# Graph attention: head 6 turned on VectorE in tiles 1 to 6, two turned heads copied by VectorE

## The chip, the core and the metric

The kernel runs on one core of a Trainium2 chip. The core has TensorE (PE; its weight loads are listed as PEld), VectorE (DVE), ScalarE (ACT), GpSimd (POOL) and SyncE (SP), each of which works through its own instructions in the order in which the program gives them; they meet at semaphores. Transfers are issued by SP and POOL and run on 16 DMA engines. The metric is the device time of one execution in microseconds (us); the verdict compares medians of runs.

## The reference

Two graph layers on x of 16 batches x 1024 nodes x 256 features, float32, with an adjacency matrix per batch. Layer 0 is masked attention with 8 heads of 32 features. Layer 1 scores pairs of nodes by one of four edge kinds.

```
h = relu(layernorm(x))
Q, K, V = h Wq' + bq, h Wk' + bk, h Wv' + bv          # 8 heads of 32
attn = softmax(where(adj == 0, -inf, Q K' / sqrt(32)))
x = x + (attn V) Wo' + bo                              # layer 0
h = relu(layernorm(x))
e_k = leaky_relu((h * a_k) h', 0.2),  k = 0..3
s = where(adj == 1, e_0, -9e15); where(adj == 2, e_1, s); ...
x = x + softmax(s) h                                   # layer 1
```

## The kernel before

**Tiles.** A tile is 128 nodes of one batch: 8 tiles a batch, 128 in all. The main loop takes one tile a turn (index s, tile t = s mod 8) and in it goes through eight stages h = 0 to 7, one head each. The order of the instructions on every engine is the order in which this loop writes them: nothing reorders them. Work of several tiles is interleaved in it: the heads of the present tile; the end of the last tile's layer 0; layer 1 of a tile nine turns back (the *edge* tile; from the tenth turn on); and the projections of a piece nine ahead.

**A head.** In stage h TensorE computes the scores of head h (`scores`, L460, two matmuls of 512 columns into PSUM). VectorE adds the mask and takes the maximum in the same instruction, into a tile `p` (`softmax_max`, L472), and reads its accumulator. In the next stage ScalarE takes the exponential, in place in `p` (`softmax_exp`, L489). In the one after, the probabilities are turned, so that the keys lie on the partitions. Heads 0 to 3 are combined with the values in stage 7 (`combine(0)`), heads 4 to 7 in stage 3 of the next turn (`combine(1)`, L524), on TensorE. Heads 6 and 7 thus have their turns in stages 0 and 1 of the next turn of the loop.

**Two ways of turning.** On TensorE: eight transpositions of 128x128 into PSUM (L588), and two copies of 128x512 into `pT` (`turn_half`, L589), by ScalarE. Or by blocks: VectorE transposes all 32x32 blocks in one instruction (`blocks_of`, L381) into a buffer `blocks`, and four transfers issued by SP (`placed`, L386, 128 KB each) put the blocks in their places in `pT`. The second way gives another order of the keys. Heads 0, 1, 4 and 5 (`MIXED`) have their values in the order that it wants, the other four in the natural order. `BY_BLOCKS` says which heads go by blocks in a tile; a tile that it does not list takes `MIXED`. Where a head's way does not agree with its values' order, the exponential does not work in place: it writes to a second `p`, with steps, so that the order comes out right (head 5 of tile 7, head 0 of tile 0).

**What is shared.** The scores of heads 4 and 6, and the edge tile's, use one PSUM side; all other heads use the other one. So scores h+1 wait, as a rule, for the maximum of head h. There are 4 buffers `p` (7 `pT`), and 3 `blocks`, given out in rotation; a buffer of `blocks` is free when the four transfers out of it have landed. The edge tile's layer 1 also goes by blocks: its probabilities (`sel`) are transposed on VectorE in stage 0, behind what the stage turns of the last tile's head 6 and ahead of stage 1's maximum.

**Stage 0 on the engines**, after the scores and the maximum of head 0: TensorE turns head 6 of the last tile, then computes the first half of the edge tile's scores (L624 transpositions, L630 matmuls; for edge tile t, between 1.9 us at t = 0 and 0.6 us from t = 4 on); VectorE transposes `sel`. In stage 1 TensorE does the scores of head 1, the turn of head 7, the turn of the normed nodes (L563) and the queries of a piece (L267); in stage 2 scores of head 2 come first. SP's transfers of stages 6 to 0 are, in order: head 4's four, a store of x (L550), head 5's four, the edge tile's four.

**Keys.** In tile 7 and tile 0 SP also loads the next batch's keys, 512 KB a head.

Of the kernel before, what the change touches and what calls it, by code (L numbers as in the profile page):

```python
# [24 lines left out]
NEG_INF = -9000000000000000.0  # L25
MASKED = -1e30
MIXED = (0, 1, 4, 5)
BY_BLOCKS = {7: (0, 1, 4), 0: (1, 4, 5)}


def by_blocks(t):
    return BY_BLOCKS.get(t, MIXED)

# [14 lines left out]
def gnn_kernel(  # L48
# [18 lines left out]
    nc = tc.nc  # L67
# [120 lines left out]
    class Piece:  # L188
# [39 lines left out]
        def turn(self):  # L228
            self.hT = self.buffer(2, [P, NC, self.n * P])
            self.hTm = self.buffer(4, [P, NC, self.n * P])  # L230
            for c in range(NC):
                if self.n > 1:
                    tr = ps_tr.tile([P, self.n, P], F32, tag="tr", name="trn0")
                elif c == 0:
                    tr = by_chunk(late)
                for t in range(self.n):
                    nc.tensor.transpose(
                        tr[:, c if self.n == 1 else t, :], self.h[:, t, c * P : (c + 1) * P], ident
                    )
                if self.n > 1:  # L240
                    nc.scalar.copy(self.hT[:, c, :], tr.rearrange("p t n -> p (t n)"))
                    nc.vector.tensor_copy(
                        self.hTm[:, c, :].rearrange("p (t k b) -> p t k b", t=self.n, b=NB),
                        tr.rearrange("p t (b k) -> p t k b", b=NB),
                    )
            self.h_ps = tr
# [168 lines left out]
    class Attend:  # L415
# [75 lines left out]
        def turn(self, h, half):  # L491
            if half == 0:
                self.turned[h] = ptp.tile([P, NT, P], F32, tag="pT", name="pT")
            turn_half(self.probs[h][0], self.turned[h], half)

        def turn_blocks(self, h):
            self.blocks = blocks_of(self.probs[h][0])
# [85 lines left out]
    def turn_half(p, pT, half, copy=nc.scalar.copy):  # L583

        tr = ps_tr.tile([P, 4, P], F32, tag="tr", name="trp")
        for j in range(4):
            jj = half * 4 + j
            nc.tensor.transpose(tr[:, j, :], p[:, jj * P : (jj + 1) * P], ident)  # L588
        copy(pT[:, half * 4 : half * 4 + 4, :], tr)  # L589
# [467 lines left out]
```

## Time and profile before

| | |
|---|---|
| median of 3 runs | 3100.66 us (3096.59 to 3105.06) |
| profiled execution | 3097.96 us, span 3096.2 us |
| granted TensorE clock | 0.992 on average |
| TensorE busy | 2943.1 us, 95% |
| VectorE, ScalarE, GpSimd busy | 2478.1, 2651.9, 2171.0 us (80%, 86%, 70%) |
| one tile, first maximum to first maximum of the next, mean of batches 1 to 14, tiles 0 to 7 | 26.1, 23.6, 23.1, 22.8, 22.6, 22.6, 22.2, 23.1 us |

A group's line reads: line of the kernel, engine, operation, output<-inputs, shape, count | busy us, mean ns of one | idle time of the engine just before them, and what ended it. A timeline's line reads: start (us from the span's start), length, engine, line, operation; in square brackets the idle time before and what released the engine. The busy time of matmuls is modelled, as they are pipelined.

### The profile page before, as it was taken

To read this page: it belongs to the slowest core of one execution; us is meant where nothing else is said; L and a number is where in the kernel's file an instruction comes from. 1 tells how busy PE (TensorE), PEld (TensorE's weight loads), DVE (VectorE), ACT (ScalarE), POOL (GpSimd) and SP (SyncE) were. 2 spreads that over 40 slices of the span, in tenths; PEclk is the share of its full clock that TensorE was granted. 3 is DMA by queue.
4 is the path that set the end of the run, shared out by engine and by line. 5 is a ranking of instruction groups with operands and counts; after the bars stand their busy time and mean duration, and the time that the engine had idled before them with its cause. 6 is when DMAs were issued, how large, how long until landed. Compare 5 with 4: busy or idle time off the path is not lost. (4 is left out here: it accounts for less than half of the span.)

```text
span 3096.2 us, 95999 instructions
## 1 busy us (share of the span) xinstructions
PE 2943.1 (95%) x36466; PEld 2211.1 (71%) x36466; DVE 2478.1 (80%) x4359; ACT 2651.9 (86%) x5221; POOL 2171.0 (70%) x2995
## 2 busy tenths in 40 slices
PE   5888999999999999999999999999999999999997
PEld 3666777777777777777777777777777777776663
DVE  3777878878787887878888788887878888787884
ACT  3888988988898988898989898898899988898882
POOL 2666777777777777777777777777777777776542
PEclk8999999999999999999999999999999999999999
DMA  5776777877778777787877878777787877778663
GB/s 203 216 237 210 225 250 229 252 219 234 251 217 275 212 235 236 236 252 227 266 219 234 257 220 272 217 230 253 227 256 225 263 226 234 253 224 255 182 175 99
DMA packets 616259, 712.44 MB, mean 230 GB/s; under 512 B 65328, under 2 KB 546992, under 8 KB 615792
## 3 DMA queue, kind: packets, MB, share of 16 engines
q1 hardware_dynamic: 546720, 494.08, 53.1%
q0 software_dynamic: 66960, 210.04, 20.9%
q8 instruction: 293, 4.80, 0.7%
q10 hardware_dynamic: 2112, 2.10, 0.2%
q14 instruction: 174, 1.43, 0.2%
HBM read 252.98 MB, written 134.22 MB: 125 GB/s over the span
## 5 line engine op out<-in xcount | busy, mean ns | idle before, releaser
L472 DVE CUSTOM_DVE_ANT_0 p<-s,neg 128x1024 f32<-128x1024 f32 x1024 | 1235.9, 1208 | 296.1 <-PE s L460 231.8
L489 ACT ACTIVATE p<-p,nmx 128x1024 f32<-128x1024 f32 x1024 | 1218.7, 1191 | 174.3 <-DVE nmx L472 172.2
L460 PE MATMUL s<-k,qt 128*128 128x512 f32 x2048 | 761.6, 453 | 70.8 <-DMA k<-kd 36.5
L589 ACT COPY pT<-trp 128x512 f32<-128x512 f32 x1088 | 581.9, 591 | 66.2 <-PE trp L588 64.1
L381 DVE STREAM_TRANSPOSE blocks<-p 128x1024 f32<-128x1024 f32 x488 | 603.9, 1238 | 14.5 <-ACT p L677 10.6
L588 PE MATMUL trp<-ident,p 128*128 128x128 f32 x4352 | 566.2, 273 | 1.7 <-ACT pT L589 1.2
L588 PEld LDWEIGHTS trp<-ident,p 128*128 128x128 f32 x4352 | 506.7, 141 | 83.3 <-ACT pT L589 9.1
L524 PE MATMUL acc<-pT,v 128*32 128x128 f32 x16384 | 536.0, 276 | 27.4 <-ACT recT L518 20.6
L524 PEld LDWEIGHTS acc<-pT,v 128*32 128x32 f32 x16384 | 456.2, 111 | 136.5 <-ACT recT L518 74.8
L440 POOL TENSOR_SCALAR neg<-adj 128x1024 bf16<-128x1024 int32 x128 | 467.7, 3654 | 80.3 <-ACT neg L452 71.1
L695 PE MATMUL acc<-h,pT 128*32 128x256 f32 x8192 | 494.7, 383 | 7.9 <-DVE ot L704 7.8
L460 PEld LDWEIGHTS s<-k,qt 128*128 128x128 f32 x2048 | 322.8, 191 | 173.9 <-issue 72.6
L695 PEld LDWEIGHTS acc<-h,pT 128*32 128x32 f32 x8192 | 241.6, 110 | 211.2 <-issue 64.4
L673 POOL TENSOR_TENSOR sel<-sel,less 128x1024 f32<-128x1024 f32 x120 | 286.8, 2390 | 76.6 <-ACT less L662 51.3
L630 PE MATMUL s<-h1T,ha 128*128 128x512 f32 (+2 forms) x744 | 272.8, 490 | 2.6 <-ACT h1T L567 1.3
L671 POOL TENSOR_SCALAR less<-top 128x1 f32<-128x1 f32 x120 | 31.6, 264 | 267.7 <-DVE top L653 267.6
L324 POOL DMA_DIRECT2D qd<-halves x240 | 177.0, 777 | 58.7 <-POOL halves L314 31.8
L489 ACT ACTIVATION_READ_ACCUMULATOR p<-p,nmx 128x1 f32 x1024 | 205.9, 201 | 0.0
L508 POOL COPY wide<-rec 128x256 f32<-128x256 f32 x128 | 53.9, 421 | 215.7 <-DVE rec L506 215.7
L330 POOL DMA_DIRECT2D kd<-halves x240 | 171.7, 764 | 35.4 <-POOL halves L314 35.4
L314 POOL TENSOR_TENSOR halves<-full,halves 128x256 fp32r<-128x256 f32 x240 | 176.4, 735 | 20.6
L630 PEld LDWEIGHTS s<-h1T,ha 128*128 128x128 f32 x744 | 126.7, 190 | 70.7 <-issue 45.0
(120 smaller groups left out, 4239.8 us busy)
## 6 DMA issues: line engine op xcount, KB each, us to landing
pT<-blocks SPq DMA_DIRECT2D x2432, 128.0 KB, 3.5
k<-kd SPq DMA_DIRECT2D x128, 512.0 KB, 6.5
qt<-qd SPq DMA_DIRECT2D x128, 512.0 KB, 4.5
adj<-in_adj POOLq DMA_DIRECT2D x127, 512.0 KB, 5.2
qd<-halves POOLq DMA_DIRECT2D x240, 256.0 KB, 3.1
kd<-halves POOLq DMA_DIRECT2D x240, 128.0 KB, 4.3
xb<-in_x POOLq DMA_DIRECT2D x128, 128.0 KB, 4.4
x1d<-x SPq DMA_DIRECT2D x128, 128.0 KB, 4.1
```

The lines of the kernel that those rows point to most:

```text
L324: nc.gpsimd.dma_start(out=qds[self.b][self.first, oc].rearrange("p u w n -> p u (w n)"), in_=halves.unsqueeze(1).to_broadcast([P, 2, 2 * P]),)
L381: nc.vector.transpose(blocks.rearrange("p b j q -> p j b q"), p)
L440: nc.gpsimd.tensor_scalar(self.neg, self.adj, 0.0, MASKED, ALU.is_equal, ALU.mult)
L460: nc.tensor.matmul(self.ps[:, cols], lhsT=self.qt[:, h, :], rhs=keysets[self.b][h][:, cols], start=True, stop=True,)
L472: nc.vector.tensor_tensor_reduce(out=p, in0=sides[h in (4, 6)], in1=self.neg, scale=-SCALE, scalar=FLOOR, op0=ALU.add, op1=ALU.min, accum_ ...
L489: nc.scalar.activation(to, of, AF.Exp, bias=nmx, scale=-1.0, accum_out=self.sums[:, h : h + 1])
L524: nc.tensor.matmul(sums_place[r * HD : (r + 1) * HD, g * P : (g + 1) * P], lhsT=vs[self.b][:, j, place_of(h) : place_of(h) + HD], rhs=self ...
L588: nc.tensor.transpose(tr[:, j, :], p[:, jj * P : (jj + 1) * P], ident)
L589: copy(pT[:, half * 4 : half * 4 + 4, :], tr)
L630: nc.tensor.matmul(self.side[:, cols], lhsT=self.ha[:, c, :], rhs=h1T[:, c, cols], start=(c == 0), stop=(c == NC - 1),)
L673: nc.gpsimd.tensor_tensor(self.sel, self.sel, self.less, ALU.subtract)
L695: nc.tensor.matmul(sums_place[a * HD : (a + 1) * HD, :], lhsT=self.pT[:, j, a], rhs=h1s[self.b][:, j, :], start=(j == 0), stop=(j == NT - 1),)
```

## The change

In tiles 1 to 6 head 6 is turned by blocks too. Its values are in the natural order, so its exponential writes to a second `p` with steps: consecutive elements go 128 bytes apart (in head 5 of tile 7 and head 0 of tile 0 they go 16 bytes apart). Head 6's eight transpositions and two copies go, in 96 tiles; a block transposition and four transfers come in their place, in stage 0 of the next turn of the loop, ahead of the edge tile's.

Where TensorE turns a head of `MIXED`, which is head 5 in tile 7 and head 0 in tile 0, VectorE makes the two copies from PSUM instead of ScalarE.

```
-BY_BLOCKS = {7: (0, 1, 4), 0: (1, 4, 5)}
+BY_BLOCKS = {7: (0, 1, 4), 0: (1, 4, 5), 1: (0, 1, 4, 5, 6), 2: (0, 1, 4, 5, 6), 3: (0, 1, 4, 5, 6), 4: (0, 1, 4, 5, 6), 5: (0, 1, 4, 5, 6), 6: (0, 1, 4, 5, 6)}
...
         def turn(self, h, half):
             if half == 0:
                 self.turned[h] = ptp.tile([P, NT, P], F32, tag="pT", name="pT")
-            turn_half(self.probs[h][0], self.turned[h], half)
+            copy = nc.vector.tensor_copy if h in MIXED else nc.scalar.copy
+            turn_half(self.probs[h][0], self.turned[h], half, copy)
```

## The prediction

> **What bounds the kernel now.** I read the page first: shares by engine, then the groups of the lines that the diff touches.
>
> ```profile
> PE 2943.1 (95%) x36466; PEld 2211.1 (71%) x36466; DVE 2478.1 (80%) x4359; ACT 2651.9 (86%) x5221; POOL 2171.0 (70%) x2995
> ...
> L489 ACT ACTIVATE p<-p,nmx 128x1024 f32<-128x1024 f32 x1024 | 1218.7, 1191 | 174.3 <-DVE nmx L472 172.2
> ...
> L589 ACT COPY pT<-trp 128x512 f32<-128x512 f32 x1088 | 581.9, 591 | 66.2 <-PE trp L588 64.1
> L381 DVE STREAM_TRANSPOSE blocks<-p 128x1024 f32<-128x1024 f32 x488 | 603.9, 1238 | 14.5 <-ACT p L677 10.6
> L588 PE MATMUL trp<-ident,p 128*128 128x128 f32 x4352 | 566.2, 273 | 1.7 <-ACT pT L589 1.2
> ```
>
> TensorE is busy for 95% and looks like the bound; taking 96 heads' turns off it would then be worth 96 x 1.04 = 100 us (566.2 / 4352 = 0.130 us a transposition, eight a head). That sum is only good if TensorE is the bound in the stretch from which the turn is taken. So the second view is the timeline of that stretch, in an ordinary tile (tile 4 of batch 5 ends, tile 5 begins; start us, length, engine):
>
> ```profile
> 1092.24 1.14 ACT L489 ACTIVATE p<-p,nmx 128x1024 f32<-128x1024 f32 x1
> 1092.26 1.23 DVE L381 STREAM_TRANSPOSE blocks<-p 128x1024 f32<-128x1024 f32 x1
> ...
> 1093.55 2.54 SPq L386 DMA_DIRECT2D pT<-blocks  x4
> ...
> 1094.53 1.24 DVE L381 STREAM_TRANSPOSE blocks<-p 128x1024 f32<-128x1024 f32 x1
> ...
> 1095.10 0.73 PE L460 MATMUL s<-k,qt 128*128 128x512 f32 x2
> ...
> 1095.67 1.04 PE L588 MATMUL trp<-ident,p 128*128 128x128 f32 x8
> ...
> 1095.96 1.23 DVE L472 CUSTOM_DVE_ANT_0 p<-s,neg 128x1024 f32<-128x1024 f32 x1 [0.19 <-issue]
> ...
> 1096.54 0.60 PE L624 MATMUL s<-ident,mirror 128*128 128x128 f32 x4
> ...
> 1097.11 1.24 DVE L381 STREAM_TRANSPOSE blocks<-sel 128x1024 f32<-128x1024 f32 x1
> 1097.25 0.30 PEld L460 LDWEIGHTS s<-k,qt 128*128 128x128 f32 x2 [0.35 <-DVE nmx L472]
> 1097.25 0.73 PE L460 MATMUL s<-k,qt 128*128 128x512 f32 x2
> ...
> 1098.28 1.19 DVE L472 CUSTOM_DVE_ANT_0 p<-s,neg 128x1024 f32<-128x1024 f32 x1
> ...
> 1099.72 0.71 PE L460 MATMUL s<-k,qt 128*128 128x512 f32 x2
> ...
> 1100.47 1.22 DVE L472 CUSTOM_DVE_ANT_0 p<-s,neg 128x1024 f32<-128x1024 f32 x1 [0.67 <-PE s L460]
> ```
>
> Here 1092.26 is the block transposition of head 4 (call it T4), 1093.55 its four transfers, 1094.53 T5, 1095.10 scores of head 0 of the new tile, 1095.67 the turn of head 6 on TensorE (the one that goes), 1095.96 the maximum of head 0, 1097.11 the edge tile's block transposition (Te), 1098.28 the maximum of head 1. Scores 0, 1 and 2 share one PSUM side, so scores 1 wait for maximum 0, and scores 2 for maximum 1. The reader is to see two things: TensorE already idles 0.35 us for maximum 0 although it has the turn of head 6 to do, and VectorE's maximum 1 begins the moment Te is done. This stretch is a chain scores - maximum - scores, not a sum of TensorE work.
>
> The third view is the line of the blocks' transfers, in the window of T4's four alone (1093.5 to 1096.1):
>
> ```profile
> DMA to landing us min/median/max: 3.5/3.7/4.1
> ```
>
> And the fourth the line of the block transpositions in the whole run, where it says until what VectorE sat idle before them (us, times):
>
> ```profile
>   DMA pT<-blocks: 2.9, 5
> ```
>
> Five times one of them waited for an older block's transfers, 2.9 us in all. The wait exists in this kernel; it is merely early enough.
>
> **Part 1: the turn of head 6 leaves TensorE (96 tiles).** It frees 1.04 us before scores 1. Scores 1 cannot start before maximum 0 ends (1097.19, against 1097.25 seen), so in tiles whose edge tile has only 0.60 us of transpositions there, the freed time becomes idle time: gain 0. Where the edge tile has more TensorE work (tiles 2 and 3), up to 1.04 us would come free, if maximum 1 were not late next, which part 2 says it is.
>
> **Part 2: VectorE gets T6, and the blocks run out.** T6 (1.24 us) stands between maximum 0 and Te. `blocks` has three buffers. Now the allocations run T4, T5, Te, T0, T1, so Te takes the buffer of the previous T1, long landed. After the change they run T4, T5, T6, Te, T0, T1: Te takes T4's buffer and must wait until all four transfers of T4 have landed (in the changed kernel's order of instructions Te waits on four DMA semaphores, those of T4's transfers). Those are issued 2.41 us before maximum 0 at 0.64 us each. In the trace's landings of the 90 tiles concerned (tiles 1 to 6, batches 1 to 15; batch 0 has no edge tiles) the last one lands 2.5 to 6.6 us after maximum 0 begins, on average 3.92, 4.20, 4.21, 4.17, 4.16, 4.15 for tiles 1 to 6. VectorE's own order would let Te start at 2.39. So Te waits, and in order behind it stands maximum 1; scores 2 and all later TensorE work wait for that.
>
> From the start of Te to the end of maximum 1's accumulator read: 1097.11 to 1099.47, 2.36 us; to scores 2 starting 0.06 (maximum 0's read ends 1097.19, scores 1 start 1097.25); to maximum 2, 0.75 (1099.72 to 1100.47). With 0.05 from landing to start (the transpositions that waited began -0.02 to 0.12 after it), maximum 2 starts at landing + 3.2: 7.1, 7.4, 7.4, 7.4, 7.4, 7.35 us after maximum 0. Now it starts after 5.09, 4.78, 4.50, 4.50, 4.50, 4.50 (trace, by tile 2 to 7). The losses are 2.0, 2.6, 2.9, 2.9, 2.9, 2.85: 16.1 us a batch, x 15 = **+242 us**. What follows scores 2 is TensorE work with hardly a gap (in this tile, 22.29 us busy of 22.40), so the delay is carried to the next tile. In batch 0 maximum 1 comes 1.24 later without a wait, which puts maximum 2 at 4.5, where it is now: 0.
>
> The transfer's price weighed against a rule: T4's 128 KB transfers took 3.5 to 4.1 us. The Trainium skill, page "SBUF — State Buffer", section "The DMA setup-cost knee", fits one as about 2 us plus bytes over 436 GB/s; that estimate is 2.3 us, the last one would land 1.8 after maximum 0, before T6 is done, and the sum would be the second rival's instead. I go by the row; the transfers share the engines with the 512 KB adjacency load issued just before.
>
> **Part 3: the exponential of head 6 writes to a second p.** Tile 7's head 5 and tile 0's head 0 have such an exponential now: 2.26 us in tile 7 against 1.14. The new one steps 128 bytes between elements where the old one steps 16. Ends: 0 (costs nothing extra) and twice the extra, 2.2 us; I take 1.12, the nearest row. Its new buffer is head 4's p (four in rotation), so it also waits for T4's end, 1.3 us later than it starts now. It then ends 0.07 after maximum 0 begins, the raising of the keys (0.61) and the exponential of head 7 behind it end at 2.05, when TensorE's turn of head 7 comes up (after scores 1, at 2.02). T6 needs it at 1.15. The cover is TensorE's wait for scores 2, at 6.6: the turn of head 7 and what follows take 2.15, so the exponential could take 4.6 us before it counted. Cost 0. The two copies that go (1.07 us a tile on ScalarE) give 0 too, as the chain does not pass through them. The raised keys reach POOL 0.65 later, beneath the same cover.
>
> **Part 4: 384 more transfers on SP.** T6's four follow T5's, as Te's do now: those land 8.8 to 12.1 after maximum 0, mean 9.73. The combination of heads 4 to 7, which now reads them, would come 10.2 to 10.7 after it (now 7.4 to 8.3, plus the loss). Mostly covered; I put 0.05 a tile, **+5 us**. Bound: 1.5 us x 90 = 135, if every one landed at the late end. Te's own transfers move 2.6 later; their reader moves as far. T0 reuses T5's buffer (landed at 7.6 on average; T0 now begins at 5.7 to 6.2 and moves to 8.3 or later), T1 reuses T6's (9.7 against 13): no wait as a rule.
>
> **Part 5: copies on VectorE in tiles 7 and 0** (64, some 0.69 us by the row of VectorE's 128x512 copies from PSUM, 688 ns). In tile 7 they follow maximum 7, and end 2.65 us after scores 7 do; maximum 0 cannot start before 3.73 (turn 1.04, combination 1.96, scores 0.73). In tile 0 they end 2.65 us after scores 2, the edge maximum behind them at 3.9, and scores 3 are there at 4.3 (turn 1.04, edge scores about 0.9, values 1.2, reciprocals 0.4, scores 0.73). ScalarE loses 1.07 a tile. Those tiles wait for keys (DMA share 0.93 and 0.86 there), so I take 0; the ends are -33 us (31 tiles x 1.07) and +44 (32 x 1.38).
>
> **Sum.** 3097.96 (the profiled execution: span 3096.2 and 1.8 around it; the median of the runs shown is 2.7 above) + 242 + 5 = **3345 us**, +8%.
>
> **Rivals.**
> First, TensorE's relief arrives: 3098 - 100 = 2998. For it: 95% busy, 22.29 of 22.40 us in the tile. It decides if maximum 1 ends before TensorE comes to scores 2, 2.7 us after maximum 0; T6 and Te alone end at 3.6. Against it is VectorE's order itself.
> Second, T4's transfers land before T6 is done (2.39), and only T6's time counts: Te at 2.39, maximum 2 at 5.6, losses 0.5, 0.8 and four times 1.1, 5.7 a batch, 3098 + 85 = 3183. For it: T4's landing comes as early as 2.5 in one tile; against it, the mean is 4.1. Between, every microsecond of landing is 90 us.
> Third, transfers also land late because there are more of them, and the combination waits: 3345 + 135 = 3480. For it: transfers of blocks have landed up to 8.8 us after issue.
> That the change turns less than it says is no case: the build has eight transpositions less on TensorE and one on VectorE more in each of the 96 tiles.
>
> **How the numbers follow.** Forecast 0.72, first rival 0.04, second 0.10, third 0.12, no change 0.02. Landings 1 us earlier or later on average make 3255 or 3435; the copies' ends lie within that. The range 3235 to 3435 leaves out most of the second and third rivals, 0.2. Within 0.3% (9 us, about what the runs, 3096.6 to 3105.1, can tell apart): 0.02. Faster 0.04, slower 0.94.
>
> **What would show it.** In the changed profile: block transpositions of `sel` idle before them, ended by `pT<-blocks` transfers, 120 to 180 us in all; TensorE's idle before scores 2, released by the maximum; busy TensorE lower by 100 us yet a longer span; tiles 2 to 7 longer by 2 to 3 us, tiles 0 and 1 unchanged; L381 at 584 on p; some 128 exponentials of 2.2 us. If Te starts without a wait, the buffer argument is wrong; if tiles 2 to 7 are shorter, the chain is.

## The result, and the profile after

The changed kernel takes 3427.54 us (3421.17 to 3438.55, four runs), the kernel before 3098.62 on the same chip: a ratio of 1.105, with a 95% interval of 1.1027 to 1.1072. The forecast was 3345 us, with a range of 3235 to 3435. The profiled execution took 3428.07 us, span 3426.2; against the profiled one of before (3097.96) that is +330 us.

The page of the changed kernel, shares and groups (the lines that answer to those shown of before, and two that have grown):

```profile
PE 3003.7 (88%) x35698; PEld 2198.6 (64%) x35698; DVE 2639.1 (77%) x4519; ACT 2618.6 (76%) x4965; POOL 2169.4 (63%) x2995
...
L489 ACT ACTIVATE p<-p,nmx 128x1024 f32<-128x1024 f32 x1024 | 1314.5, 1285 | 465.6 <-DVE nmx L472 344.7
...
L460 PE MATMUL s<-k,qt 128*128 128x512 f32 x2048 | 771.7, 459 | 346.6 <-DVE nmx L472 291.7
...
L381 DVE STREAM_TRANSPOSE blocks<-p 128x1024 f32<-128x1024 f32 x584 | 723.0, 1238 | 11.5 <-ACT p L678 10.6
...
L589 PE MATMUL trp<-ident,p 128*128 128x128 f32 x3584 | 467.7, 274 | 1.8 <-ACT pT L590 1.0
...
L381 DVE STREAM_TRANSPOSE blocks<-sel 128x1024 f32<-128x1024 f32 x120 | 149.3, 1244 | 134.4 <-DMA pT<-blocks 134.1
```

The work moved as written: TensorE's transpositions are 98.5 us lighter (566.2 to 467.7), VectorE's block transpositions 119 us heavier. What is new is in the right-hand columns. VectorE stands idle for 134 us before the edge tile's block transposition until transfers of blocks have landed, and TensorE stands idle for 347 us before the scores (71 before), 292 of them for a maximum. The same two groups before:

```profile
L460 PE MATMUL s<-k,qt 128*128 128x512 f32 x2048 | 761.6, 453 | 70.8 <-DMA k<-kd 36.5
...
L381 DVE STREAM_TRANSPOSE blocks<-sel 128x1024 f32<-128x1024 f32 x120 | 148.8, 1240 | 0.0
```

One line speaks against the forecast: TensorE's busy time rose by 61 us, although 98 us of work left it.

The same stretch as in the prediction, in the timeline of the changed kernel (end of tile 6 of batch 5, begin of tile 7; the maximum of head 0 starts at 1261.72):

```profile
1259.25 2.25 ACT L489 ACTIVATE p<-p,nmx 128x1024 f32<-128x1024 f32 x1 [1.17 <-DVE blocks L381]
...
1261.84 1.16 ACT L489 ACTIVATE p<-p,nmx 128x1024 f32<-128x1024 f32 x1
...
1262.88 1.24 DVE L381 STREAM_TRANSPOSE blocks<-p 128x1024 f32<-128x1024 f32 x1
...
1263.01 0.73 PE L460 MATMUL s<-k,qt 128*128 128x512 f32 x2 [1.03 <-DVE nmx L472]
...
1263.58 1.03 PE L589 MATMUL trp<-ident,p 128*128 128x128 f32 x8
...
1267.46 1.25 DVE L381 STREAM_TRANSPOSE blocks<-sel 128x1024 f32<-128x1024 f32 x1 [3.34 <-DMA pT<-blocks]
1268.63 1.19 DVE L472 CUSTOM_DVE_ANT_0 p<-s,neg 128x1024 f32<-128x1024 f32 x1
...
1269.88 0.79 PE L460 MATMUL s<-k,qt 128*128 128x512 f32 x1 [4.16 <-DVE nmx L472]
```

The line of the blocks' transfers, in the window of head 4's four (1259.0 to 1262.2):

```profile
DMA to landing us min/median/max: 4.0/5.0/6.4
```

Read from the top: the exponential of head 6 waits for head 4's block transposition and takes 2.25 us; head 6's own block transposition (T6, 1262.88) follows maximum 0; the edge tile's (Te) then waits 3.34 us; maximum 1 starts when it is done, and TensorE has waited 4.16 us for it. This is a tile with late transfers, shown because of what comes next. Two windows, the tile before and this one (length, then busy us and count of PE, PEld, DVE, ACT and POOL, then the granted TensorE clock, the DMA share and GB/s):

```profile
1237.07:1261.72 24.65, 21.77 (x278) 16.18 (x276) 20.61 (x35) 20.10 (x39) 15.74 (x21) 1.00 0.75 223
1261.72:1291.40 29.68, 24.49 (x286) 19.10 (x285) 20.82 (x37) 21.48 (x41) 20.38 (x30) 0.88 0.82 247
```

The granted clock is the share of TensorE's full clock that the trace records. In the long tile it is 0.88 on average: the record has it at 0.5 (half clock) from 1267.9 on, for 6.8 us. Tile by tile, 48 of the 89 tiles that have both T6 and Te (batches 1 to 15; the last one is not counted, having no successor) contain a stretch at half clock; before the change none of these tiles did.

### The profile page after: what moved, and what is told of

It is laid out like the page before. It is cut to its first block, busy times and chain, and to the rows that moved or that the text cites. A ratio compares the mean times of both kernels' runs of the same rounds, so it can differ in the third digit from the quotient of the medians.

```text
span 3426.2 us, 95002 instructions
## 1 busy us (share of the span) xinstructions
PE 3003.7 (88%) x35698; PEld 2198.6 (64%) x35698; DVE 2639.1 (77%) x4519; ACT 2618.6 (76%) x4965; POOL 2169.4 (63%) x2995
## 5 line engine op out<-in xcount | busy, mean ns | idle before, releaser
L489 ACT ACTIVATE p<-p,nmx 128x1024 f32<-128x1024 f32 x1024 | 1314.5, 1285 | 465.6 <-DVE nmx L472 344.7
L460 PE MATMUL s<-k,qt 128*128 128x512 f32 x2048 | 771.7, 459 | 346.6 <-DVE nmx L472 291.7
L381 DVE STREAM_TRANSPOSE blocks<-p 128x1024 f32<-128x1024 f32 x584 | 723.0, 1238 | 11.5 <-ACT p L678 10.6
L460 PEld LDWEIGHTS s<-k,qt 128*128 128x128 f32 x2048 | 324.5, 193 | 480.4 <-DVE nmx L472 353.6
L525 PE MATMUL acc<-pT,v 128*32 128x128 f32 x16384 | 558.3, 277 | 19.5 <-ACT recT L519 10.3
L525 PEld LDWEIGHTS acc<-pT,v 128*32 128x32 f32 x16384 | 471.7, 111 | 135.0 <-ACT recT L519 62.6
L590 ACT COPY pT<-trp 128x512 f32<-128x512 f32 x832 | 443.1, 587 | 59.1 <-PE trp L589 58.0
L589 PE MATMUL trp<-ident,p 128*128 128x128 f32 x3584 | 467.7, 274 | 1.8 <-ACT pT L590 1.0
L589 PEld LDWEIGHTS trp<-ident,p 128*128 128x128 f32 x3584 | 418.7, 141 | 70.0 <-ACT pT L590 8.9
L631 PE MATMUL s<-h1T,ha 128*128 128x512 f32 (+2 forms) x744 | 332.0, 576 | 2.6 <-ACT h1T L568 0.5
L381 DVE STREAM_TRANSPOSE blocks<-sel 128x1024 f32<-128x1024 f32 x120 | 149.3, 1244 | 134.4 <-DMA pT<-blocks 134.1
L631 PEld LDWEIGHTS s<-h1T,ha 128*128 128x128 f32 x744 | 146.8, 218 | 91.6 <-issue 61.2
```

The costliest lines, as they stand in the source:

```text
L381: nc.vector.transpose(blocks.rearrange("p b j q -> p j b q"), p)
L460: nc.tensor.matmul(self.ps[:, cols], lhsT=self.qt[:, h, :], rhs=keysets[self.b][h][:, cols], start=True, stop=True,)
L489: nc.scalar.activation(to, of, AF.Exp, bias=nmx, scale=-1.0, accum_out=self.sums[:, h : h + 1])
L525: nc.tensor.matmul(sums_place[r * HD : (r + 1) * HD, g * P : (g + 1) * P], lhsT=vs[self.b][:, j, place_of(h) : place_of(h) + HD], rhs=self ...
L631: nc.tensor.matmul(self.side[:, cols], lhsT=self.ha[:, c, :], rhs=h1T[:, c, cols], start=(c == 0), stop=(c == NC - 1),)
```

## Where the 330 us are

From the trace, by tile, batches 1 to 15:

| | forecast | measured |
|---|---|---|
| tiles 2 to 7, maximum 0 to maximum 2, now 6.9 to 7.4 us (before 4.5 to 5.1) | +242 | 15.5 us a batch, +232 |
| tiles 2 to 7, maximum 2 to the next tile | 0 | 6.0 us a batch, +90 |
| the waits of the combination (part 4) | +5 | hardly there: L525 waits 10.9 us for transfers (9.7 of them in batch 0), 10.3 before (L524) |
| tiles 0 and 1 | 0 | -8 and +1 |
| batch 0 | 0 | +15 |

The first line is the forecast's mechanism at the forecast's size. The second was not in the sum. In tiles whose clock stayed at 1.0, the part after maximum 2 takes 18.25 us on average; in the 48 with half clock 19.75; before it took 18.05. So the half clock goes with 48 x 1.5 = 72 of the 90 us; the other 0.2 us a tile stay open.

The edge tile's score matmuls are one place where the half clock falls, in stage 2 behind the wait. By shape, their 512-column group before,

```profile
L630 PE MATMUL s<-h1T,ha 128*128 128x512 f32 x376 | 178.1, 596 | 2.6 <-ACT h1T L567 1.3
```

and after:

```profile
L631 PE MATMUL s<-h1T,ha 128*128 128x512 f32 x376 | 221.7, 722 | 2.6 <-ACT h1T L568 0.5
```

The same 376 matmuls are busy 44 us longer. So TensorE can be busier with less to do.

## The experiments

The times of before, run beside them, were 3106.9 us in the first group (the first four), 3102.6 in the second (four) and 3106.1 in the third (two).

**e1_copies: the copies alone.**

```
-BY_BLOCKS = {7: (0, 1, 4), 0: (1, 4, 5), 1: (0, 1, 4, 5, 6), ... 6: (0, 1, 4, 5, 6)}
+BY_BLOCKS = {7: (0, 1, 4), 0: (1, 4, 5)}
```

> Only the copies of part 5 change: VectorE makes them for head 5 in tile 7 and head 0 in tile 0; BY_BLOCKS is that of before. My theory: hidden, 0, at most the 0.5 us by which tile 0 is shorter in the changed kernel (26.0 to 25.5), so 3085 to 3105 us against 3099 before. Rival, that the copies lengthen VectorE's chain: 32 pairs x 1.38 = +44, 3143 us.

Measured: 3109.9 us (12 runs) against 3106.9, a ratio of 0.9995 (0.9973 to 1.0016). The copies took what the nearest row said, as the group's line shows:

```profile
L590 DVE COPY pT<-trp 128x512 f32<-128x512 f32 x64 | 41.1, 683 | 0.0
```

Neither VectorE's 41 us nor ScalarE's relief reaches the end. The bounds in us were missed by 5, but before itself is 8 us higher in this group than when they were written; the ratio answers the question.

**e2_blocks4: the changed kernel with four buffers of blocks.**

```
-blocks = work.tile(..., tag="blocks", bufs=3);  ptp bufs=7
+blocks = work.tile(..., tag="blocks", bufs=4);  ptp bufs=6
```

> The changed kernel with four buffers of blocks instead of three (and six pT instead of seven, to make room). My theory, the buffer: the edge tile's transposition no longer waits for transfers, starts 2.4 us after maximum 0, maximum 2 comes at 5.6, TensorE's idle stretch is short enough that the clock stays up: 3099 + 85 = 3184 us, at most 3210. Rival, that VectorE's added work, the stepped exponential or the added transfers cost most: still over 3380. If six pT are too few, the combination (L525) waits and the line says so.

Measured: 3258.2 us, a ratio of 1.049 (1.046 to 1.053), 169 us below the changed kernel. Te starts 2.3 us after maximum 0, maximum 2 comes at 5.46 (5.6 forecast), and one tile of the 89 has a stretch of half clock. But 3258 is above 3210. The waits of the block transpositions for transfers are gone, in the line of L381,

```profile
  DMA pT<-blocks: 2.7, 2
```

and the combination has got one, in the line of L525:

```profile
  DMA pT<-blocks: 72.3, 89
```

With scores 2 earlier, the combination of heads 4 to 7 comes before head 6's own transfers have landed. That is the prediction's third rival, which the wait for the buffer had covered. The combination reads transfers of heads 4, 5 and 6; the trace says which it waited for: 88 of the 89 waits end within 0.3 us of the landing of one of head 6's. These are issued as soon after T6 as in the changed kernel (1.7 us), so the six pT do not hold them up; that six pT cost something elsewhere can't be excluded.

**e3_before_blocks2: the wait alone, in the kernel before.**

```
-blocks = work.tile(..., tag="blocks", bufs=3)
+blocks = work.tile(..., tag="blocks", bufs=2)
```

> The kernel before with two buffers of blocks instead of three: nothing is moved between engines, but the edge tile's transposition takes head 4's buffer, as in the changed kernel. My theory: it waits until head 4's transfers have landed, maximum 2 comes at 7.1 to 7.4 us after maximum 0, some 240 us in all, and less of the half clock than in the changed kernel, as TensorE still has 1.04 us more work there: 3330 to 3390 us. Rival, that the wait for the buffer is not what costs: 3090 to 3110.

Measured: 3452.2 us (two runs), a ratio of 1.111. Nothing was moved between engines, and the kernel is as slow as the changed one. The line of L381:

```profile
  DMA pT<-blocks: 240.6, 80
```

66 of these waits, 210 us, stand before Te in tiles 2 to 7. So the buffer's wait is enough by itself. The size was missed by 60 us: maximum 2 comes at 7.5 to 7.8 us after maximum 0, later than expected (head 4's transfers land at 4.2 on average, against 3.8 in the changed kernel), and the half clock did not become less (granted clock 0.959 on average).

**e4_in_place: no second p for head 6.**

```
-if (h in MIXED) != (h in by_blocks(self.t)):
+if h != 6 and (h in MIXED) != (h in by_blocks(self.t)):
```

> The changed kernel, but head 6's exponential works in place in tiles 1 to 6, with no second p and no steps (head 6's keys are then in the wrong order against its values). My theory: the exponential is hidden under TensorE's wait, so the time stays at that of the changed kernel, 3415 to 3440 us. Rival, that the exponential's length and its wait for head 4's p make the 85 us that the forecast lacked: 3340 to 3370.

Measured: 3450.9 us (3434.1 and 3467.7), 11 us above the expected bounds and on the far side from the rival. Taking away 1.1 us of ScalarE's time and a wait in 96 tiles brings nothing. Part 3's "cost 0" holds.

**e5_fill8 and e6_fill16: idle TensorE is given unread work.** Eight transpositions of the identity in stage 0, in the place of the turn that left; in the second kernel eight more at the end of stage 1.

```
+def fill():
+    tr = ps_tr.tile([P, 4, P], F32, tag="tr", name="fill")
+    for j in range(4):
+        nc.tensor.transpose(tr[:, j, :], ident, ident)
...
+if h == 0 and was and 6 in by_blocks(was.t):   # before the edge tile's scores
+    fill(); fill()
...
+    fill(); fill()                              # e6 alone: in stage 1, after the projection
```

> The changed kernel plus eight transpositions of the identity on TensorE in stage 0, where the turn of head 6 was; nobody reads them. They are added work of 1.04 us in 96 tiles, in a stretch where TensorE waits. If TensorE's relief were worth anything there, +100: 3530 us. My theory, no worth, and the half clock comes from TensorE's idle stretch: not slower, and with less idle time fewer half-clock windows, 3370 to 3425 us. Rival, the half clock has nothing to do with the idle stretch: 3420 to 3440 with as much half clock as in the changed kernel (273 us).

> As the run before, plus eight more such transpositions in stage 1, after the queries' projection, where TensorE waits for maximum 1: 2.08 us of added work in 96 tiles. My theory: the idle stretch before scores 2 falls below some 1.5 us in most tiles, the clock stays up, the rest of the tile after maximum 2 takes 18.1 us instead of 19.1, so some 80 us come back: 3335 to 3375 us, in spite of 200 us more TensorE work. Rival, the half clock costs nothing in the chain: 3420 us or more.

Measured: 3429.7 us (3427.6 and 3431.9) and 3369.2 (3368.8 and 3369.6). The first: 100 us of TensorE work put back cost nothing, so in the changed kernel its removal is worth nothing; but it did not help either, against my expectation. The idle time before scores 1 was filled, the longer one before scores 2 was not, and 44 of 89 tiles still had half clock. The second: with 200 us more TensorE work than the changed kernel it is 58 us faster. Tiles with half clock fell from 48 to 13. The clock lines of the changed kernel,

```profile
core 0: 3426.2 us, clock 0.960
```

and of e6_fill16:

```profile
core 0: 3367.0 us, clock 0.985
```

The clock records have 273 and 106 us at half clock. Maximum 2 hardly moved (7.0 to 7.3 us after maximum 0), the rest of the tile went from 19.1 to 18.4. So the idle time costs more than its own length: it makes the work after it slower.

**e7_edge_later: the edge tile's transposition behind maximum 1.**

```
                 if h == 0:
...
-                    edge_was.turn_blocks()
-                    edge_was.place_blocks()
                 if h == 1:
+                    if edge_was:
+                        edge_was.turn_blocks()
+                        edge_was.place_blocks()
```

> The changed kernel with the edge tile's block transposition and its transfers moved behind maximum 1 (from stage 0 to stage 1), three buffers as they are. It still waits for head 4's transfers, but maximum 1 no longer stands behind it. My theory: maximum 1 starts 2.4 us after maximum 0, scores 2 come as before the change, and the next thing that is late shows: the combination of heads 4 to 7 waits for head 6's own transfers (landing at about 9.7 against a start at 7.8), up to 2 us in 90 tiles: 3180 to 3280 us. Rival, that the added work on VectorE alone is the cost: 3380 or more.

Measured: 3281.5 us (3274.3 and 3288.7), just past the upper end of what was expected. Maximum 1 starts 2.31 us after maximum 0 (2.37 before the change), though Te still waits, and the combination's line (L525) has

```profile
  DMA pT<-blocks: 116.1, 104
```

All 104 waits end within 0.3 us of a landing of head 6's. Same rival, shown a second time and from another side: here too, taking the first wait away uncovers head 6's own transfers. The line's wait for the turned reciprocals (recT, copied by ScalarE) grew as well, to 151 us from 95 before the change; no run separates what that costs.

**e8_combine_later, e9_unblocked, e10_project_early: an attempt to keep TensorE's gain.** The combination of heads 4 to 7 goes from stage 3 to stage 4, so that head 6's transfers can land; then what that blocked is put right; then the queries' projection is moved into stage 0.

```
 # e8, on top of e7
-h == 3: was.combine(1); ...; was.combined()
-h == 4: was.output()      h == 5, before its maximum: was.residual(); norms(was, piece_nxt)
+h == 4: was.combine(1); was.combined()
+h == 5, before gather(0): was.output(); was.residual(); norms(was, piece_nxt)
 # e9, on top of e8
-h == 3: edge_was.load_nodes()      h == 4: piece.normed()
+h == 4, after combined: edge_was.load_nodes()      h == 5, after norms: piece.normed()
 # e10, on top of e9
-h == 1: piece_was.project(1, 0); piece_was.project(1, 1)
+h == 0, after edge.score(0): piece_was.project(1, 0); piece_was.project(1, 1)
```

> As the run before, and the combination of heads 4 to 7 moved from stage 3 to stage 4 (with it the product with the reciprocals; the output projection, the residual and the norms move from stages 4 and 5 to stage 5). Head 6's transfers then have one more stage to land. My theory: the last new wait is gone, and the kernel comes back to that of before, with part of TensorE's 1.04 us a tile: 3030 to 3130 us. Rival, the moved steps make a wait of their own (residual, norms, store): 3150 to 3250.

> As the run before (combination of heads 4 to 7 in stage 4), with what that move blocked put right: the piece's norm on ScalarE, which shares a buffer with the combined heads, goes from stage 4 to stage 5, behind the output projection, and GpSimd's load of the edge tile's nodes, which shares one with the reciprocals, from stage 3 to stage 4. My theory: ScalarE's and GpSimd's long waits (410 and 471 us) go, the combination hardly waits for transfers (3 us), and the kernel comes to 3050 to 3160 us. Rival, that the later combination itself makes the tile longer: over 3200.

> As e9_unblocked, and the piece's query projection moved on TensorE from stage 1 to stage 0, before scores 1, where TensorE waits for maximum 0. If TensorE's idle there (some 1 us a tile) is what keeps the 1.04 us from being worth anything, this is 30 to 80 us faster than e9_unblocked; if VectorE's chain of maximum 0, head 6's transposition and maximum 1 sets scores 2, it changes nothing (within 15 us).

Measured: 3666.8, 3564.6 and 3597.5 us; all three missed. In e8 the combination's wait for transfers is down to 3.0 us, as meant, but among the longest waits stands

```profile
ACT h L223 <- PE acc L540: 410.5, 118, 4.8
```

The piece's norm writes the buffer that the output projection still reads, and ScalarE queues behind it. e9 cures that. What stays is a wait that e8 has too (368.6 us there):

```profile
PEld s L460 <- ACT mirror L645: 359.4, 105, 4.7
```

Scores 4 need the PSUM side that the edge tile's scores hold until ScalarE has copied them. In the kernel before, L460 waits 12.4 us for this copy. By the order of the instructions, the combination in stage 3 is the work that covers it there, and moved behind scores 4 it leaves the wait bare; no run tests that alone. e10 gains nothing on top (33 us slower), so filling TensorE's idle time before scores 1 does not bring the 1.04 us back. No version beat the kernel before.

## Why the prediction was right, and where a term was missing

The time lies within the range, 7 us below its upper end, and that is luck. The margin above 3345 had been set for landings 1 us later; they came 0.4 us earlier (3.8 us after maximum 0 on average, 4.1 forecast). What filled the margin was the half clock, which stood in no sum: +330 us against +247. Two of the signs that the prediction named did not come: TensorE's busy time rose by 61 us instead of falling by 100, and tiles 2 to 7 became 3.2 to 4.2 us longer, not 2 to 3.

- **What bounds the kernel.** Right: the stretch is a chain scores - maximum - scores, and TensorE's 95% did not make the turn's removal worth anything. e5_fill8 shows it for the changed kernel; no run takes the turn away without giving it to VectorE. One reading was off: the 0.35 us of idle time before scores 1 is that of the weight load's row. The matmuls paused 0.11 us there (L624 ends at 1097.14, scores 1 start at 1097.25).
- **Part 2, the blocks.** Right in place, and in size with two small errors that offset each other: the landings came 0.4 us early, and from landing to maximum 2 it took 3.45 us on average, not 3.2. VectorE idles 134 us before Te for transfers (120 to 180 forecast), maximum 2 comes 6.9 to 7.4 us after maximum 0 (7.1 to 7.4), +232 of +242 us. e3_before_blocks2 shows that the wait alone makes the kernel this slow, and e2_blocks4 that without it maximum 2 comes at 5.46.
- **"The delay is carried to the next tile", with nothing added.** This is the term that was missing. The prediction let TensorE idle for 2 to 3 us and priced what follows by the rows of a TensorE that had not idled. After the wait 48 of 89 tiles run at half clock for a while and take some 1.5 us longer, 72 of the +90 us; e6_fill16 gets 58 us back by filling idle time alone. The kernel before had no half clock in these tiles, yet its page had the price elsewhere: its granted clock was 0.992, not 1.
- **Part 3.** Right: 2.2 us an exponential (the group's mean rose from 1191 to 1285), hidden.
- **Part 4.** Right at the forecast's place only because part 2's wait covered it: the third rival's wait is real and shows as soon as the cover goes (72 us in e2_blocks4, 116 in e7_edge_later). Its reason, that transfers land later because there are more of them, does not show: head 6's landed 9.2 us after maximum 0 on average in the changed kernel (9.73 forecast), and 9.4 and 9.5 in these two; it is the combination that comes earlier there. Batch 0, which has no edge tiles and so no such cover, is where it showed in the changed kernel itself. Its part 2 was forecast at 0 and came to +15 us (163.3 to 178.8 for its eight tiles). A line of its timeline, the combination of heads 4 to 7 in the turn of tile 2:

```profile
113.29 2.81 PE L525 MATMUL acc<-pT,v 128*32 128x128 f32 x60 [1.88 <-DMA pT<-blocks]
```

  The prediction looked there at the maxima alone and not at the transfers. The combination waits 9.7 us for them in this batch (before it had no such wait there), and the time at half clock rose from 6.1 to 20.2 us. With the combination a stage later (e8_combine_later) batch 0 takes 163.5 us again.
- **Part 5.** Right: 0.

The skill's rule for the transfers, weighed in the prediction (the Trainium skill, page "SBUF — State Buffer", section "The DMA setup-cost knee"), would have given the second rival, 3183 us. The landings of head 4's transfers in the changed kernel were 2.1 to 6.1 us after maximum 0, and the row of before was the better guide.

## What to carry to other kernels

When work is moved to another engine, count the buffers that it takes from their rotation as well as its time: here 1.24 us of VectorE put maximum 2 back by 0.4 to 1.0 us (e2_blocks4), and the one buffer of three by another 1.5 to 1.9, as it put a wait for transfers ahead of an instruction that TensorE waits for. A wait that goes uncovers the next one that is late, so each repair has to be followed through to the resource that it hands over earlier. And a busy share near 100% prices nothing until the stretch is known: TensorE's turn was worth nothing in a kernel that was 95% TensorE, as the stretch that it left waited for VectorE.

## What had not been expected of the hardware

A TensorE that waits a few microseconds comes back slower. In the tile shown above it idled 1.03 and then 4.16 us, and the granted clock was 0.5 for 6.8 us. Tiles with half clock have maximum 2 at 7.5 to 8.3 us after maximum 0 (means by tile), those without at 6.4 to 6.6, so the longer waits bring it more often; e6_fill16, which shortens the idle time and not the wait, has a quarter of these tiles.

The changed kernel's clock record says more closely when. Every stretch at half clock begins on one grid of 3.41 us steps, and all but the last one last a whole number of steps. After the first 20 us, of the steps at full clock in which TensorE was busy (by its modelled matmuls) for less than 45%, all 52 were followed by half clock; of those busy for more than 50%, 1 of 826; of those in between, 4 of 19. The other eleven traces divide in the same place, with few exceptions. So it took no unbroken idle time of a step's length: in the tile shown, the step before the drop (1264.5 to 1267.9) was 37% busy. A wait of a middling length can thus bring the half clock or not, by where it falls on the grid.

The Trainium skill, page "TensorE: Matmul & The Clock Gate", section "Part 1: The HAM clock gate", tells of a clock that halves after an idle window of about 3.4 us. The length agrees with the steps of the record; the condition does not, as a step that was partly busy was enough here. The page calls the penalty of warming up less than 1% of a typical span, in a passage on how a kernel begins. Here it recurs in every second tile: the +90 us above, nearly 3% of the kernel, were mostly its doing, and 58 us came back with the idle time filled.
